# Loading the taps of a 3x3 convolution onto other partitions: four transfers of two taps for am, two for an, some to every second partition

## The chip, the cores and the metric

The kernel runs on one core of a Trainium2 chip. The metric is device time in microseconds of one execution. Five engines matter here: TensorE (PE, with its weight loads PEld), VectorE (DVE), ScalarE (ACT), GpSimd (POOL) and SyncE (SP), which only starts transfers. All transfers are carried by the core's 16 DMA engines.

## What is computed

Four images of 16 channels, 256 x 256, float32, pass through two layers. Each layer adds to its input a function of the group-normalised input (`_gn`, 8 groups).

```python
# layer 0
out = conv3x3(gn(x), conv_w) + conv_b            # 16 -> 400 channels: 16 channels x 25 logits
w   = softmax(out.reshape(N, 16, 25, H, W), axis=2)
x   = x + sum over the 25 taps of unfold5x5(gn(x)) * w
# layer 1
x   = x + silu(patches3x3(gn(x))) @ base_w + b_splines(patches3x3(gn(x))) @ spl_w + bias
```

The change is in layer 0, in how the operands of the 3x3 convolution reach the chip's memory.

## The kernel before, in words

**Setup (0 to 110 us).** The images are read once for their statistics. Meanwhile the first half of image 0 is normalised and written to DRAM three times: as `hs` (rows, for the 5x5 window), as `hst` (columns, float32) and as `hsl`, which holds for each channel two planes `[C, 2, CT]`: the value rounded to float32r (`hi`) and what the rounding lost (`lo`). `prepare0` lays out the weights: `wm` (float32, 128 rows: 8 of the 9 taps x 16 channels) and `wn` (float32r, 97 rows: the ninth tap, and the bias).

**Layer 0 (110 to 2021 us).** There are 64 strips of 32 image columns (`SW`), each worked through in 4 tiles of 8 columns (`CI`), so 256 tiles; and a tile in 2 units of 4 columns (`JG`), so 512 units.

- For each tile `load_im` starts on SP three transfers into `am` (lines 717 to 724: 48, 48 and 32 partitions, each row a run of 1038 floats) and two into `an` (lines 727 to 734: 32 partitions each, the 16 channels times hi and lo, the same source twice). The rows of `am` are 8 shifted copies of 16 channels. Rows 64 to 96 of `an` hold ones (line 706), which multiply the bias rows of `wn`.
- For each column PE multiplies 128 rows of `am` by `wm` (line 922) and 97 rows of `an` by `wn` (line 926) into the same PSUM bank `lg` (400 logits).
- ACT takes the exponential of two columns at a time (line 945) into `e`.
- POOL multiplies `e` by the 5x5 window `u` (line 950), one instruction per unit.
- DVE sums both over the 25 taps (line 771), one instruction per unit. Per strip it then makes the quotient (lines 791, 795, 799, with ACT's Ln and Exp at 785 and 787), and POOL subtracts it from `xc` (line 805).
- After every four strips ACT starts two stores of 1 MB each, `x1s<-xc` (line 862), in rows of 512 bytes; there are 15 such pairs on ACT, the last is on POOL.
- Between the units, steps of `normalize` prepare the next image in the same way (transposes at line 402, ACT's copies, `lo` on DVE at line 414, the writes at lines 323 and 337).

**What sets the order.** The program of each engine is fixed when it is built. `load_im(k + 2)` stands at the start of tile k; `am` has three buffers, so the load of a tile waits until PE has finished the tile three before. SP is one queue in order: `am`, `an`, `u` (five transfers a strip, line 743), `xc` (line 749), `xp` (line 315) and the writes stand behind each other. In the built program every transfer of SP and of ACT carries one of eight completion semaphores, taken in turn in program order, ACT's stores included. A transfer is not started until the last one on its semaphore, eight places earlier, has landed. So SP has at most eight transfers in flight, and the pair of stores holds two of the eight places until it has landed.

**Layer 1 (2021 to 2912 us)** reads `x1s` and is not touched.

Of the kernel before, what the change touches and what calls it, by code (L numbers as in the profile page):

```python
# [34 lines left out]
def conv_preact_kernel(  # L35
# [32 lines left out]
    LAG = 1  # L68
    RP = P + 2
    CT = (W + 2) * RP  # L70
    QC = 4
    QW = W // (P // QC)
    QG = 4
# [26 lines left out]
    ident = const.tile([P, P], F32, name="ident")  # L100
# [7 lines left out]
    for k, d in enumerate((0, RD - 1)):  # L108
        h = k * (P // 2)
# [142 lines left out]
    zero = const.tile([PAD * C, max(RP, NST * SP)], F32, name="zero")  # L252
    nc.vector.memset(zero, 0.0)

    zpad = const.tile([P, QC, PAD], F32, name="zpad")
    nc.vector.memset(zpad, 0.0)

    def zeros(b, queue):

        for e in (0, HP - PAD):  # L260
            for r in range(PAD):
                yield partial(
                    queue.dma_start,
                    hs[b][:, e + r].rearrange("s c w -> c s w"),
                    zero[0:C, 0 : NST * SP].rearrange("c (s w) -> c s w", s=NST),
                )
        yield partial(
            queue.dma_start,
            bass.AP(
                tensor=x1s[b].tensor, offset=x1s[b].offset,  # L270
                ap=[[CP, C], [(H + 1) * W, 2], [1, W]],
            ),
            zero[0 : 2 * C, 0:W],
        )
        for h in range(NH):
            for w in (0, (W + 1) * RP):
                yield partial(queue.dma_start, hst[b][h][:, w : w + RP], zero[0:C, 0:RP])
                yield partial(
                    queue.dma_start,
                    hsl[b][h][:, :, w : w + RP].rearrange("c t r -> (c t) r"), zero[:, 0:RP],  # L280
                )


# [2 lines left out]
    kept = [  # L286
        const.tile([P, C // QC * NQ, QG, 1], d, name=f"kept{i}") for i, d in enumerate((F32, F32R, F32R))
    ]

    def normalize(b, ptr, tiles, held=None, copier=None, part=None, dense=False):  # L290
# [22 lines left out]
        def load(q, h):  # L313
            if held is None and q < C // QC:
                nc.sync.dma_start(
# [13 lines left out]
        def put_columns(q, n):  # L329
            g0 = n * QG  # L330
            for h in parts:

                for to, ti, t in ((hst, 0, tts[n]), (hsl, 0, his[n]), (hsl, 1, los[n])):
                    d = to[b][h]
                    m = 2 if to is hsl else 1
                    t = t if t.dtype == F32 else t.bitcast(F32)
                    nc.sync.dma_start(
                        bass.AP(
                            tensor=d.tensor,
                            offset=d.offset + q * QC * m * CT + ti * CT + (1 + g0) * RP,  # L340
                            ap=[[QW * RP, W // QW], [m * CT, QC], [1, QG * RP]],
                        ),
                        t[:, h].rearrange("p g r -> p (g r)"),
                    )
# [115 lines left out]
    with tc.tile_pool(name="prep0", bufs=2) as prep, tc.tile_pool(  # L460
        name="pre", bufs=1
    ) as pre, tc.tile_pool(
        name="xin", bufs=3
    ) as xin, tc.tile_pool(name="stat", bufs=2) as stat, tc.tile_pool(
        name="pstat", bufs=1, space=PSUM
# [16 lines left out]
        loaded = [load_x(n) for n in range(5)]  # L482

        wr = pre.tile([P, NL], F32, name="wr")
        for dj in range(3):
            v = conv_wt[dj].rearrange("(d c) n -> c d n", d=3)
            nc.sync.dma_start(
                wr[dj * 3 * C : min((dj + 1) * 3 * C, P), :], v[:, 0 : 3 if dj < 2 else 2, :]
            )
        wnr = pre.tile([KT, NL], F32, name="wnr")  # L490
        nc.vector.memset(wnr, 0.0)
        v = conv_wt[2, 2 * C : 3 * C]
        for r in (0, 2 * C):
            nc.sync.dma_start(
                wnr[r : r + 2 * C, :],
                bass.AP(tensor=v.tensor, offset=v.offset, ap=[v.ap[0], [0, 2], [1, NL]]),
            )
        for r in (4 * C, 6 * C):
# [4 lines left out]
        for d in range(3):  # L503
# [3 lines left out]
            v = spl_s[dc]  # L507
# [23 lines left out]
        def prepare0():  # L531

            def places(t):
                return t.rearrange("p (c m d) -> p m c d", c=C, m=K)

            wp = pre.tile([KT, K, C, K], F32, name="wp")
            for m in range(K):
                nc.gpsimd.tensor_copy(wm[:, m], places(wr)[:, m])
                nc.gpsimd.tensor_copy(wp[:, m], places(wnr)[:, m])
            whi = pre.tile([KT, K, C, K], F32R, name="whi")  # L540
# [13 lines left out]
            nc.vector.memset(times[0 : 4 * C], 0.25)  # L554
            nc.vector.memset(times[4 * C : 4 * C + 1], 1.0)
# [41 lines left out]
        for b in range(B):  # L597
            st = stat.tile([P, G, NH * (GC if b == 0 else 1), 6], F32, name=f"st0_{b}", tag=f"st0{min(b, 1)}")
            for hf in range(NH):
                n = b * NH + hf  # L600
                t = loaded.pop(0)
# [33 lines left out]
            v = hm[:, b * NH : (b + 1) * NH]  # L635
# [55 lines left out]
    def layer0(shift):  # L691
# [4 lines left out]
        with tc.tile_pool(name=f"prep{arm}", bufs=2) as prep, tc.tile_pool(  # L696
            name=f"im{arm}", bufs=NIM
        ) as imp, tc.tile_pool(name=f"l0{arm}", bufs=2) as l0, tc.tile_pool(
            name=f"nd{arm}", bufs=3
        ) as ndp, tc.tile_pool(name=f"x1{arm}", bufs=3) as x1p, tc.tile_pool(name=f"ptr{arm}", bufs=1, space=PSUM) as ptr, tc.tile_pool(  # L700
            name=f"plog{arm}", bufs=3, space=PSUM
        ) as plog, tc.tile_pool(name=f"prc{arm}", bufs=1, space=PSUM) as prc:
            ans = [imp.tile([KT, CI * RP], F32R, name=f"an{n}{arm}", bufs=1) for n in range(NIM)]
            for t in ans:

                nc.vector.memset(t.bitcast(F32)[4 * C : KT], 1.0)
            tiles = norm_tiles(prep)
            strips = [(b, hf, s) for b in range(B) for hf in range(NH) for s in range(NST)]
            nci = SW // CI
# [1 line left out]
            def load_im(n):  # L711
                b, hf, s = strips[n // nci]
                j0 = s * SW + n % nci * CI
                run = CI * RP - 2
                am = imp.tile([P, CI * RP], F32, name=f"am{n}{arm}", tag="am")
                d = hst[b][hf]
                for dj in range(3):
                    nd = 3 if dj < 2 else 2
                    nc.sync.dma_start(
                        am[dj * 3 * C : dj * 3 * C + nd * C, 0:run],  # L720
                        bass.AP(
                            tensor=d.tensor, offset=d.offset + (j0 + dj) * RP,
                            ap=[[CT, C], [1, nd], [1, run]],
                        ),
                    )
                an = ans[n % NIM]
                d = hsl[b][hf]
                for r in (0, 2 * C):
                    nc.sync.dma_start(
                        an.bitcast(F32)[r : r + 2 * C, 0:run],  # L730
                        bass.AP(
                            tensor=d.tensor, offset=d.offset + (j0 + 2) * RP + 2,
                            ap=[[CT, 2 * C], [1, run]],
                        ),
                    )
                return am, an
# [118 lines left out]
            def store(n, xc):  # L855
# [5 lines left out]
                for h in range(2):  # L861
# [7 lines left out]
                    name=nc.get_next_instruction_name(), engine=mybir.EngineType.Activation,  # L869
# [10 lines left out]
            for n, (b, hf, s) in enumerate(strips):  # L880
# [22 lines left out]
                nd = ndp.tile([P, 2, C, SW], F32, name=f"nd_{n}{arm}", tag="nd")  # L903
                for j in range(0, SW, JG):
                    if j % CI == 0:
                        k = n * nci + j // CI
                        if k + 2 < len(strips) * nci:
                            ims.append(load_im(k + 2))
                        am, an = ims.pop(0)
# [8 lines left out]
                    for j1 in range(0, JG, 2):  # L918
# [28 lines left out]
                        tensor=u.tensor, offset=u.offset + j,  # L947
                        ap=[u.ap[0], [1, JG], [SP, K * C], [1, K]],
# [436 lines left out]
```

## Time and profile before

| | us |
|---|---|
| median of 4 runs | 2912.2 |
| lowest, highest run | 2910.28, 2913.88 |
| profiled execution, its own time | 2913.87 |
| its span (first to last instruction) | 2912.0 |
| setup, up to the first transfer of layer 0 | 109.6 |
| last convolution matmul starts | 2021.0 |
| transfers of am: 512 of 194.6 KB, 256 of 129.8 KB | SP issue, median 0.587 |
| transfers of an: 512 of 129.8 KB | SP issue, median 0.422 |

The profile is of one execution. A group's row gives line, engine, operation, output<-inputs, count, busy time, mean duration, and the idle time just before its instructions with what ended it. A row of the table by stretches gives for each engine the busy time in that stretch and the number of instructions, then the granted TensorE clock (1.00 is full), the mean busy share of the 16 DMA engines (it can exceed 1 in a short stretch, because a packet is booked where it ends) and the GB/s that they moved.

### The profile page before, as it was taken

How to read it: one execution, taken by the hardware profiler on the slowest of the kernel's cores; microseconds unless marked ns; L12 is line 12 of the kernel's file. 1: busy time of each engine (PE TensorE's matmuls, PEld its weight loads, DVE VectorE, ACT ScalarE, POOL GpSimd, SP SyncE). 2: the span in 40 equal slices, each digit the busy share in tenths (PEclk: the TensorE clock that was granted, in tenths of full speed). 3: DMA queues.
4: the chain of work that ended last, by engine and by line, in shares of the span. 5: the costliest groups of instructions: out<-in, count | busy, mean ns of one | idle time of the engine just before them, and what ended most of it. 6: DMA issues, size and time to landing. Idle time of an engine off the chain costs nothing.

```text
span 2912.0 us, 40991 instructions
## 1 busy us (share of the span) xinstructions
PE 2719.1 (93%) x14282; PEld 1507.5 (52%) x14282; DVE 2803.6 (96%) x1866; ACT 2124.8 (73%) x2764; POOL 2704.1 (93%) x1117
## 2 busy tenths in 40 slices
PE   4699999999999999999999999997799999999998
PEld 3466656666666656656656656664243343333232
DVE  6599999999999999999999999999899999999996
ACT  6466876667767558676655655647899999999995
POOL 4299999999999999999999999999899999999995
PEclk7799999999999999999999999999899999999999
DMA  9898999889889688888976757766788788787883
GB/s 283 242 247 229 258 250 269 238 216 241 234 235 256 192 218 235 236 236 233 252 205 172 201 160 195 193 173 176 247 245 259 243 256 250 243 263 240 256 249 101
DMA packets 403467, 664.43 MB, mean 228 GB/s; under 512 B 43186, under 2 KB 267908, under 8 KB 387380
## 3 DMA queue, kind: packets, MB, share of 16 engines
q1 hardware_dynamic: 339284, 626.53, 76.6%
q10 hardware_dynamic: 61920, 31.46, 3.8%
q0 software_dynamic: 2048, 3.72, 0.4%
q8 instruction: 117, 1.92, 0.3%
q14 instruction: 98, 0.80, 0.1%
HBM read 532.96 MB, written 121.15 MB: 225 GB/s over the span
## 4 chain that ended last, share of the span: by engine, by line
DVE 44%; PE 27%; DMA 9%; ACT 7%; issue 6%; POOL 5%; SPq 2%; DVEq 0%; ACTq 0%; POOLq 0%
DVE nd L771 32%; PE lg L922 12%; PE yp L1252 9%; PE lg L926 3%; DVE ring L175 3%; POOL e L950 3%; DVE s L172 3%; PE yp L1261 2%; DMA an<-hsl 2%; DMA x1s<-xc 2%; DVE r1a L1096 1%; ACT xta L1087 1%; DMA xin<-in_x_dram 1%; ACT xtb L1087 1%; DMA xta<-x1s 1%
## 5 line engine op out<-in xcount | busy, mean ns | idle before, releaser
L950 POOL TENSOR_TENSOR e<-e,u 128x1600 f32<-128x1600 f32 x512 | 1788.8, 3544 | 54.4 <-ACT e L945 40.1
L922 PE MATMUL lg<-wm,am 128*128 128x400 f32 x4096 | 1736.6, 505 | 74.8 <-ACT e L945 36.7
L771 DVE TENSOR_REDUCE nd<-e 128x128 f32<-128x3200 f32 x512 | 1760.7, 3484 | 34.6 <-POOL e L950 34.1
L926 PE MATMUL lg<-wn,an 97*128 97x400 f32 x2048 | 1344.2, 656 | 15.0 <-DMA an<-hsl 14.8
L945 ACT ACTIVATE e<-lg 128x800 f32<-128x800 f32 x1024 | 834.5, 839 | 580.4 <-PE lg L926 329.2
L922 PEld LDWEIGHTS lg<-wm,am 128*128 128x128 f32 x4096 | 763.7, 192 | 387.5 <-ACT e L945 70.1
L1252 PE MATMUL yp<-ring,wt 128*32 128x512 f32 x6144 | 721.1, 595 | 35.4 <-DVE ring L175 34.9
L926 PEld LDWEIGHTS lg<-wn,an 97*128 97x128 f32 x2048 | 388.6, 190 | 336.5 <-DMA an<-hsl 25.2
L1252 PEld LDWEIGHTS yp<-ring,wt 128*32 128x32 f32 x6144 | 234.4, 109 | 485.9 <-issue 397.2
L1109 POOL TENSOR_TENSOR s1b<-s1b,r1a 128x1024 f32<-128x1024 f32 (+1 forms) x96 | 192.5, 2038 | 0.0
L1109 POOL TENSOR_TENSOR s1a<-s1a,r1a 128x1024 f32<-128x1024 f32 (+1 forms) x96 | 192.1, 2032 | 0.0
L175 DVE SCALAR_TENSOR_TENSOR ring<-s,s1a 128x1024 f32<-128x1024 f32 x132 | 156.7, 1211 | 0.9
L825 ACT ACTIVATE z<-xc,nrm 128x256 f32<-128x256 f32 x240 | 144.0, 600 | 18.2 <-POOL xc L805 14.2
L175 DVE SCALAR_TENSOR_TENSOR ring<-s,s1b 128x1024 f32<-128x1024 f32 (+1 forms) x128 | 153.6, 1225 | 0.3
L1109 POOL TENSOR_TENSOR s1a<-s1a,r1b 128x512 f32<-128x512 f32 (+2 forms) x68 | 119.4, 1781 | 0.0
L1109 POOL TENSOR_TENSOR s1b<-s1b,r1b 128x512 f32<-128x512 f32 x64 | 114.8, 1819 | 0.0
L1105 POOL TENSOR_TENSOR s1a<-r1b 128x1536 f32<-128x1536 f32 (+1 forms) x31 | 86.6, 2793 | 28.3 <-ACT r1b L1094 28.3
L172 DVE SCALAR_TENSOR_TENSOR s<-xta,cb,s 128x1024 f32<-128x1024 f32 (+2 forms) x90 | 112.3, 1274 | 0.3 <-DMA sla<-x1s 0.2
L172 DVE SCALAR_TENSOR_TENSOR s<-xtb,cb,s 128x1024 f32<-128x1024 f32 (+2 forms) x85 | 107.1, 1287 | 3.8 <-ACT s L169 3.8
L172 DVE SCALAR_TENSOR_TENSOR s<-xtc,cb,s 128x1024 f32<-128x1024 f32 (+2 forms) x85 | 107.0, 1286 | 0.0
L169 ACT ACTIVATE s<-xta,cb 128x1024 f32<-128x1024 f32 (+2 forms) x90 | 96.4, 1085 | 12.4 <-DVE ring L175 10.8
L1105 POOL TENSOR_TENSOR s1b<-r1b 128x1536 f32<-128x1536 f32 (+1 forms) x32 | 86.3, 2698 | 18.6 <-ACT r1b L1094 18.6
(209 smaller groups left out, 2313.1 us busy)
## 6 DMA issues: line engine op xcount, KB each, us to landing
am<-hst SPq DMA_DIRECT2D x512, 194.6 KB
u<-hs SPq DMA_DIRECT2D x320, 288.0 KB
an<-hsl SPq DMA_DIRECT2D x512, 129.8 KB
xta<-x1s SPq DMA_DIRECT2D x40, 1024.0 KB
xtb<-x1s SPq DMA_DIRECT2D x40, 1024.0 KB
xtc<-x1s SPq DMA_DIRECT2D x40, 1024.0 KB
am<-hst SPq DMA_DIRECT2D x256, 129.8 KB
x1s<-xc ACTq DMA_DIRECT2D x30, 1024.0 KB
```

The lines of the kernel that those rows point to most:

```text
L169: nc.scalar.activation(s, t, AF.Square, scale=-0.5, bias=cb)
L172: nc.vector.scalar_tensor_tensor(p, t, cb2, s, ALU.subtract, ALU.mult)
L175: nc.vector.scalar_tensor_tensor(f, p, 0.0, q, ALU.min, op)
L771: nc.vector.tensor_reduce(nd[:, :, :, j : j + JG].rearrange("p t c j -> p t j c"), e.rearrange("p t j m c d -> p t j c m d"), AX.XY, ALU.add,)
L825: nc.scalar.activation(z, v, f, scale=nrm[b][:, 0, g : g + 1], bias=nrm[b][:, 1, g : g + 1], accum_out=st1[b][:, t, g, columns_of(n) : col ...
L922: nc.tensor.matmul(lg[:, i, :NL], lhsT=am[:, o : o + P], rhs=wm.rearrange("p m c d -> p (m c d)"), start=True, stop=False,)
L926: nc.tensor.matmul(lg[:, i, :NL], lhsT=an[:, o : o + P], rhs=wn.rearrange("p m c d -> p (m c d)"), start=False, stop=True,)
L945: nc.scalar.activation(ev, lg[:, :, :NL], AF.Exp)
L950: nc.gpsimd.tensor_tensor(e[:, 1].rearrange("p j m c d -> p j (m c) d"), e[:, 0].rearrange("p j m c d -> p j (m c) d"), uv, ALU.mult,)
L1105: nc.gpsimd.tensor_tensor(s1(n, a, z), r1(n, a, z), r1(n, a, z), ALU.mult)
L1109: nc.gpsimd.tensor_tensor(s1(n, a, z), s1(n, a, z), r1(n, a, z), ALU.mult)
L1252: nc.tensor.matmul(yp[t * M : (t + 1) * M], lhsT=wt[:, d, e].rearrange("p r o -> p (r o)"), rhs=ring[:, r0 + t * RT + d : r0 + t * RT + d ...
```

## The change

`am` is loaded by four transfers of two taps (32 partitions each) where there were three of 48, 48 and 32. The first goes to partitions 0 to 31, the third to 96 to 127, the second and the fourth to the even and the odd ones of 32 to 95. `an` still takes two transfers of 32 partitions, now to the even and the odd partitions of 32 to 95, and its ones are rows 0 to 31; it has 96 rows, not 97. `hsl` has a pitch of 2 CT + 16 floats for each channel, so that its source keeps a dimension of 16 channels and one of 2 planes. The rows of the weights and of the bias follow: `wr` is loaded by four transfers, `wnr` by two of another shape, and `wn` is made by two instructions on DVE (a rounding copy, and `whi * odd + wp`, where `odd` is -1 on odd partitions), where it took one on DVE and three on ACT. In layer 0 the number of instructions on PE, ACT, POOL and DVE is unchanged; SP starts six transfers for each tile, not five.

```diff
+    CL = 2 * CT + 16
...
-    hsl = [[dram.tile([C, 2, CT], F32, name=f"hsl{b}_{h}") for h in range(NH)] for b in range(B)]
+    hsl = [[dram.tile([C, CL], F32, name=f"hsl{b}_{h}") for h in range(NH)] for b in range(B)]
...
-    KT = 6 * C + 1
+    KT = 6 * C
+    TAPS = (
+        (slice(0, 2 * C), (0, 0), (0, 1)),
+        (slice(2 * C, 6 * C, 2), (1, 0), (0, 1)),
+        (slice(6 * C, P), (0, 2), (1, 0)),
+        (slice(2 * C + 1, 6 * C, 2), (2, 0), (0, 1)),
+    )
...
             whi = pre.tile([KT, K, C, K], F32R, name="whi")
-            nc.scalar.copy(whi, wp)
-            nc.vector.tensor_sub(wn, wp, whi.bitcast(F32))
-            nc.scalar.copy(wn[0 : 2 * C], wp[0 : 2 * C])
-            nc.scalar.copy(wn[4 * C : 4 * C + 1], wp[4 * C : 4 * C + 1])
+            nc.vector.tensor_copy(whi, wp)
+            nc.vector.scalar_tensor_tensor(
+                wn, whi.bitcast(F32), odd[0:KT], wp, ALU.mult, ALU.add
+            )
...
-                nc.vector.memset(t.bitcast(F32)[4 * C : KT], 1.0)
+                nc.vector.memset(t.bitcast(F32)[0 : 2 * C], 1.0)
...
-                for dj in range(3):
-                    nd = 3 if dj < 2 else 2
+                for rows_, at, step in TAPS:
                     nc.sync.dma_start(
-                        am[dj * 3 * C : dj * 3 * C + nd * C, 0:run],
+                        am[rows_, 0:run],
                         bass.AP(
-                            tensor=d.tensor, offset=d.offset + (j0 + dj) * RP,
-                            ap=[[CT, C], [1, nd], [1, run]],
+                            tensor=d.tensor, offset=d.offset + (j0 + at[0]) * RP + at[1],
+                            ap=[[CT, C], [step[0] * RP + step[1], 2], [1, run]],
                         ),
                     )
                 an = ans[n % NIM]
                 d = hsl[b][hf]
-                for r in (0, 2 * C):
+                for k in range(2):
                     nc.sync.dma_start(
-                        an.bitcast(F32)[r : r + 2 * C, 0:run],
+                        an.bitcast(F32)[2 * C + k : 6 * C : 2, 0:run],
                         bass.AP(
                             tensor=d.tensor, offset=d.offset + (j0 + 2) * RP + 2,
-                            ap=[[CT, 2 * C], [1, run]],
+                            ap=[[CL, C], [CT, 2], [1, run]],
                         ),
                     )
```

More of the change, by code (lines that the diff above doesn't have):

```diff
@@ L279, in zeros @@
                     queue.dma_start,
-                    hsl[b][h][:, :, w : w + RP].rearrange("c t r -> (c t) r"), zero[:, 0:RP],
+                    hsl[b][h][:, 0 : 2 * CT].rearrange("c (t w) -> c t w", t=2)[:, :, w : w + RP],
+                    zero[:, 0:RP],
                 )
@@ L334, in put_columns @@
                     d = to[b][h]
-                    m = 2 if to is hsl else 1
+                    pitch = CL if to is hsl else CT
                     t = t if t.dtype == F32 else t.bitcast(F32)
@@ L339, in put_columns @@
                             tensor=d.tensor,
-                            offset=d.offset + q * QC * m * CT + ti * CT + (1 + g0) * RP,
-                            ap=[[QW * RP, W // QW], [m * CT, QC], [1, QG * RP]],
+                            offset=d.offset + q * QC * pitch + ti * CT + (1 + g0) * RP,
+                            ap=[[QW * RP, W // QW], [pitch, QC], [1, QG * RP]],
                         ),
@@ L484, in conv_preact_kernel @@
         wr = pre.tile([P, NL], F32, name="wr")
-        for dj in range(3):
-            v = conv_wt[dj].rearrange("(d c) n -> c d n", d=3)
+        for rows_, at, step in TAPS:
             nc.sync.dma_start(
-                wr[dj * 3 * C : min((dj + 1) * 3 * C, P), :], v[:, 0 : 3 if dj < 2 else 2, :]
+                wr[rows_],
+                bass.AP(
+                    tensor=conv_wt.tensor,
+                    offset=conv_wt.offset + (at[0] * 3 + at[1]) * C * NL,
+                    ap=[[NL, C], [(step[0] * 3 + step[1]) * C * NL, 2], [1, NL]],
+                ),
             )
@@ L492, in conv_preact_kernel @@
         v = conv_wt[2, 2 * C : 3 * C]
-        for r in (0, 2 * C):
+        for r in (2 * C, 4 * C):
             nc.sync.dma_start(
                 wnr[r : r + 2 * C, :],
-                bass.AP(tensor=v.tensor, offset=v.offset, ap=[v.ap[0], [0, 2], [1, NL]]),
+                bass.AP(
+                    tensor=v.tensor, offset=v.offset + (r // C - 2) // 2 * (C // 2) * NL,
+                    ap=[[NL, C // 2], [0, 4], [1, NL]],
+                ),
             )
-        for r in (4 * C, 6 * C):
+        for r in range(2):
             nc.sync.dma_start(wnr[r : r + 1, :], conv_b)
@@ L539, in prepare0 @@
                 nc.gpsimd.tensor_copy(wp[:, m], places(wnr)[:, m])
+            odd = pre.tile([P, 1], F32, name="odd")
+            nc.vector.reduce_sum(odd, ident[:, 1:P:2], AX.X)
+            nc.vector.tensor_scalar(odd, odd, -1.0, None, ALU.mult)
             whi = pre.tile([KT, K, C, K], F32R, name="whi")
-            nc.scalar.copy(whi, wp)
-            nc.vector.tensor_sub(wn, wp, whi.bitcast(F32))
-            nc.scalar.copy(wn[0 : 2 * C], wp[0 : 2 * C])
-            nc.scalar.copy(wn[4 * C : 4 * C + 1], wp[4 * C : 4 * C + 1])
+            nc.vector.tensor_copy(whi, wp)
+            nc.vector.scalar_tensor_tensor(
+                wn, whi.bitcast(F32), odd[0:KT], wp, ALU.mult, ALU.add
+            )
             aw = pre.tile([P, 2, NL], F32, name="aw")
@@ L553, in prepare0 @@
             nc.vector.memset(times, 0.0)
-            nc.vector.memset(times[0 : 4 * C], 0.25)
-            nc.vector.memset(times[4 * C : 4 * C + 1], 1.0)
+            nc.vector.memset(times[2 * C : 4 * C], 0.25)
+            nc.vector.memset(times[4 * C : 6 * C], 0.25)
+            nc.vector.memset(times[0:1], 1.0)
             nc.tensor.matmul(wps, lhsT=onec, rhs=aw[:, 0], start=True, stop=False)
@@ L716, in load_im @@
                 d = hst[b][hf]
-                for dj in range(3):
-                    nd = 3 if dj < 2 else 2
+                for rows_, at, step in TAPS:
                     nc.sync.dma_start(
-                        am[dj * 3 * C : dj * 3 * C + nd * C, 0:run],
+                        am[rows_, 0:run],
                         bass.AP(
-                            tensor=d.tensor, offset=d.offset + (j0 + dj) * RP,
-                            ap=[[CT, C], [1, nd], [1, run]],
+                            tensor=d.tensor, offset=d.offset + (j0 + at[0]) * RP + at[1],
+                            ap=[[CT, C], [step[0] * RP + step[1], 2], [1, run]],
                         ),
@@ L727, in load_im @@
                 d = hsl[b][hf]
-                for r in (0, 2 * C):
+                for k in range(2):
                     nc.sync.dma_start(
-                        an.bitcast(F32)[r : r + 2 * C, 0:run],
+                        an.bitcast(F32)[2 * C + k : 6 * C : 2, 0:run],
                         bass.AP(
                             tensor=d.tensor, offset=d.offset + (j0 + 2) * RP + 2,
-                            ap=[[CT, 2 * C], [1, run]],
+                            ap=[[CL, C], [CT, 2], [1, run]],
                         ),
```

## The prediction

> **What bounds the kernel now.** I read the page first, for each engine's share and its dearest groups; then layer 0 in stretches, to see which engine has no time left; then the waits of that engine and of the one before it.
>
> ```profile
> PE 2719.1 (93%) x14282; PEld 1507.5 (52%) x14282; DVE 2803.6 (96%) x1866; ACT 2124.8 (73%) x2764; POOL 2704.1 (93%) x1117
> ...
> L950 POOL TENSOR_TENSOR e<-e,u 128x1600 f32<-128x1600 f32 x512 | 1788.8, 3544 | 54.4 <-ACT e L945 40.1
> ...
> L771 DVE TENSOR_REDUCE nd<-e 128x128 f32<-128x3200 f32 x512 | 1760.7, 3484 | 34.6 <-POOL e L950 34.1
> ```
>
> One unit costs POOL 3.544 us and DVE 3.484; with what each strip adds, both are near full. The stretches of layer 0 (after the span and the PE and PEld columns comes DVE, then ACT, POOL, clock, DMA share, GB/s):
>
> ```profile
> 110.00:150.00 40.00, 31.27 (x95) 19.66 (x96) 20.90 (x10) 16.58 (x23) 21.81 (x15) 0.82 1.01 241
> 150.00:500.00 350.00, 337.42 (x1213) 219.69 (x1211) 348.97 (x148) 248.17 (x432) 338.98 (x104) 0.99 0.93 250
> 500.00:900.00 400.00, 385.95 (x1364) 249.84 (x1363) 398.78 (x163) 269.64 (x463) 393.65 (x123) 0.99 0.86 233
> 900.00:1300.00 400.00, 378.21 (x1317) 243.17 (x1315) 396.60 (x161) 261.46 (x458) 386.94 (x121) 0.98 0.86 229
> 1560.00:1990.00 430.00, 409.72 (x1412) 263.67 (x1410) 424.87 (x186) 242.10 (x390) 429.37 (x142) 0.99 0.71 186
> ```
>
> After 150 us DVE is busy 99% of the time, and after 1560 POOL is (429.37 of 430). DMA is full only at the start. The waits of DVE and POOL from 150 to 1990 say how much a faster load can return at all:
>
> ```profile
> DVE nd L771 <- POOL e L950: 15.6, 15, 2.5
> ...
> POOL e L950 <- ACT e L945: 35.6, 21, 6.1
> ```
>
> DVE idles 15.6 us in 1840, and 18.8 us more before 150. So whatever the change does to the DMA engines, layer 0 can gain 34 us at the very most, and only where these idle times come from loads.
>
> **What a tile's load costs now.** Two stretches, one with only `u` in flight (128 partitions), one with only `am` and `an` (32 to 48), and the SP rows of that tile:
>
> ```profile
> 1898.00:1900.50 2.50, 2.50 (x11) 1.61 (x10) 2.50 (x2) 1.56 (x2) 2.50 (x2) 1.00 1.06 393
> 1908.00:1910.00 2.00, 2.00 (x8) 1.27 (x7) 2.00 (x3) 1.29 (x2) 2.00 (x2) 1.00 1.03 237
> ```
> ```profile
> 1905.76 1.81 SPq L719 DMA_DIRECT2D am<-hst  x3
> 1907.67 0.99 SPq L729 DMA_DIRECT2D an<-hsl  x2
> ```
>
> The DMA engines are full in both, yet move 393 GB/s in one and 237 in the other, though the rows of `am` are longer (4152 bytes against 2304). The number of partitions is the difference that I see. A tile is 2 x 194.6 + 129.8 + 2 x 129.8 = 778.6 KB, 797 kB, so 3.36 us at 237 GB/s. **After:** six transfers of 132.9 kB. Those to 32..95 in steps of two spread over 64 partitions. If these four go at 393 and the other two at 237: 4 x 0.34 + 2 x 0.56 = 2.47 us, 0.9 less. Bounds: all six at 393 is 2.03 us, 1.3 less; nothing gained, and the sixth transfer adding its issue time of 0.60, is 0.6 more. I take 0.9, since `u` with 288 KB a transfer is the nearest row to an unshared load.
>
> The trace shows that few partitions are slow, not which partitions share a way in. The Trainium skill, "SBUF — State Buffer", section "Door 1: The DMA port swizzle", says which: 0 to 31 reach 8 of 16 ports, 0 to 63 the same 8, 64 to 127 the others; so rows 32 to 95 reach all 16, and two rows for each DMA engine, four partitions apart from the next engine's, would give each its own port. Against the change stands the same page's "The DMA setup-cost knee": each transfer pays some 2 us, and few large ones are better. By that, paid in turn, 256 more transfers would be an estimate of 512 us; the five transfers that take 3.36 us together at a DMA share of 1.03 say that it isn't paid in turn.
>
> SP: three transfers 1.81 us, 0.60 each, with a source of three dimensions; two 0.99, 0.50 each, with two. Now all have three: 4 x 0.60 + 2 x 0.60 = 3.6 us against 2.8, so 0.8 more a tile, 205 us in all. Its cover:
>
> ```profile
> SPq L719 <- PE lg L926: 475.9, 180, 5.8
> ...
> SPq L729 <- DMA x1s<-xc: 73.1, 10, 14.5
> SPq L719 <- DMA x1s<-xc: 65.2, 17, 11.1
> ```
>
> SP waits 476 us for PE to release buffers, twice what is added. Where that cover is gone (SP catching up), 0.8 us a tile shows and takes back the 0.9. Behind a late issue stand `u`, `xc` and the writes of `normalize`.
>
> **Step 1, setup.** ACT loses three instructions on `whi` and `wn` (0.51, 0.52 and 0.53 us at 53 to 57 us), DVE gets two for one (nearest row: its `wn` at 55.56, 0.55 us). ACT is busy 10.00 of 10 us from 60 to 70 and from 70 to 80, and SP's last image load (issued at 80.13, landed at 91) stands behind ACT's work; the chain of waits runs through `ACT wn L544`. All of it returned is -1.6; DVE's two on the chain instead, +1.1. I take -1.0. One more `wr` transfer stands behind image loads that take to 37 us, and `wm` is first touched at 44: nothing.
>
> **Step 2, the start, 110 to 150.** Before the first matmul stand one more issue of 0.60 and two of 0.1: PE starts 0.8 later. But DMA is the bound here (1.01), and DVE's second stall (4.57 us at 137) comes from ACT, which waits 5.51 us in order for `xp` to land at 135.45, behind two further tiles in the queue. 2 x 0.9 less: -1.8, and the later start disappears in that stall. Ends: +0.8 (loads no faster), -3.5 (three tiles at 1.3 are 3.9, less some issue).
>
> **Step 3, the rest of layer 0.** I went through DVE's idle times one by one.
> - At 468 to 475 (0.9), 824 to 839 (1.2) and 1303 to 1318 (2.6) they end a catch-up: DMA share 1.04 from 786 to 821, in which SP starts five tiles. 5 x 0.9 = 4.5 us of the 4.8 and 6.1 that POOL idles there. I take 3.8 of the 4.7 as returned.
> - At 1041 to 1050 (3.2) and 1520 to 1528 (2.5) SP was held by a pair of stores:
>
> ```profile
> 1015.54 2.15 ACTq L862 DMA_DIRECT2D x1s<-xc  x2
> 1020.74 0.52 SPq L337 DMA_DIRECT2D hst<-tt  x1
> 1024.43 1.86 SPq L719 DMA_DIRECT2D am<-hst  x3
> 1030.42 1.67 PE L922 MATMUL lg<-wm,am 128*128 128x400 f32 x2 [6.13 <-DMA am<-hst]
> 1037.78 7.00 POOL L950 TENSOR_TENSOR e<-e,u 128x1600 f32<-128x1600 f32 x2 [6.13 <-ACT e L945]
> ```
>
> SP goes on at 1020.74, when the first store has landed, and at 1024.43 after the second; only then is the tile's load started. In the changed program one write more is held until the second store (0.6), and the six issues take 0.8 longer; the data come 0.9 sooner. I count 0.
> - From 1716 to 1737 (4.9) POOL is busy throughout and sets the pace: 0.
> - **New holds.** In the program before, at 7 of the 15 pairs the first store holds an `an` load of the next tile, the second only an `am` of the tile after. In the changed program there the second store holds the next tile itself. At 1620.48 `an` is issued after the first store and lands at 1626.8; after the second (the `am` row from 1622.13 takes 4.66 us, its last two issues 1.2 of it, so about 1625.6) and with nothing beside it, landing 2.3 us after issue (as at the start: 113.64 to 115.9), it would be 1627.9: 1.1 late. ACT's exponentials were then only 0.2 to 0.4 us ahead of POOL (done at 1632.22 for a unit that starts at 1632.6), after the store at 1853 2.5 us. Four of these pairs lie where POOL sets the pace. I take +1.0 in all; ends 0 and 7 x 3.7 = 26 (the 3.7 us between 1020.74 and 1024.43, uncovered).
>
> Step 3: -3.8 + 1.0 = -2.8. **Sum: -1.0 - 1.8 - 2.8 = -5.6 us**, so 2908.3 for the profiled execution (2913.87: span 2912.0 and 1.9 around it). The median is 1.7 below that execution, so 2906.6. Layer 1 is untouched.
>
> **Rivals.**
> 1. *The cover is gone everywhere.* The catch-ups and the holds vanish too, and all of setup and start comes back: -1.6 - 3.5 - (15.6 - 4.9) = -15.8, 2896.4. For it: DMA work falls by 256 x 0.9 = 230 us. Against it: the holds are no matter of bandwidth (DMA stood still from 1012 to 1016).
> 2. *The loads get no faster*, since rows or queues and not partitions make 237 GB/s: start +0.8, setup -1.0, catch-ups +0.8 a tile on SP, some 3 us: 2915. Against it: the row at 393 with shorter rows.
> 3. *Slower: the stores hold the next tile.* Place: the seven pairs. It decides once the second store lands over 2.5 us (the larger margin seen) after PE needs the tile. Price 7 x (1.1 to 3.7) = 8 to 26, less the 6.6 of steps 1, 2 and the catch-ups that stay: +1 to +19, middle 2922. For it: ACT's margin of 0.2 to 0.4 us at 1632. Against it: earlier pairs have DVE, not POOL, as the pace, with 1 us more of margin.
>
> **How the numbers follow.** Forecast (2903 to 2910) 0.52; rival 1 (2894 to 2903) 0.16; rival 2 (2911 to 2916) 0.15; rival 3 (2914 to 2932) 0.17. About 0.2% (5.8 us, to 2906.4) is what a measurement can tell from no change; half of the forecast's range lies past it. Faster: 0.26 + 0.16 = 0.42; same: 0.26 + 0.15 = 0.41; slower: 0.17. The range leaves out the far half of rival 3 and the lowest of rival 1: 2896 to 2919.
>
> **What would show it.** With only `am` and `an` in flight: 300 GB/s or more at a share of 1 (wrong if 237). Six issues in 3.6 us. DVE's wait for POOL from 150 to 1990 about 12 us; at 820 and 1300 none, at 1040 and 1520 still there. `xp` landing 1 to 2 us sooner after the first load. The last image load issued near 79. If POOL waits for ACT after 1560 at each fourth strip, rival 3 is at work; if `an` is what PE waits for there, by these holds.

## The result, and the profile after

The changed kernel takes **2914.7 us** (median of 33 runs, 2910.81 to 2920.51) where the kernel before takes 2910.6 (53 runs): a ratio of 1.0012, 95% interval 1.0008 to 1.0017. The forecast was a gain of 5.6 us; it is a loss of 4.1. The profiled execution of the changed kernel took 2917.7 us (span 2915.4), against 2913.9 (2912.0).

The page's two dearest groups after the change:

```profile
L968 POOL TENSOR_TENSOR e<-e,u 128x1600 f32<-128x1600 f32 x512 | 1789.5, 3550 | 61.1 <-ACT e L963 47.2
...
L789 DVE TENSOR_REDUCE nd<-e 128x128 f32<-128x3200 f32 x512 | 1761.2, 3481 | 38.5 <-POOL e L968 37.6
```

The work of one unit is what it was (3.55 and 3.48 us). The idle time in front of it has grown, from 54.4 to 61.1 us on POOL and from 34.6 to 38.5 on DVE. Three of the stretches of layer 0 (columns as before: PE, PEld, DVE, ACT, POOL, clock, DMA share, GB/s; a packet's whole time is booked in the stretch in which the packet starts):

```profile
150.00:500.00 350.00, 334.02 (x1198) 217.88 (x1198) 345.69 (x147) 245.12 (x429) 335.72 (x104) 0.99 0.83 247
500.00:900.00 400.00, 386.71 (x1347) 251.18 (x1345) 394.66 (x162) 267.88 (x459) 388.98 (x122) 0.97 0.77 231
...
1560.00:1990.00 430.00, 411.10 (x1401) 263.66 (x1400) 423.66 (x185) 241.62 (x384) 427.46 (x141) 0.98 0.63 182
```

The DMA engines move about as many GB/s as before (247, 231 and 182 for 250, 233 and 186), in less busy time: the share falls from 0.93, 0.86 and 0.71 to 0.83, 0.77 and 0.63. That looks as hoped, but `c_contig` below, without the spread, shows the same fall. And DVE has lost 3.3 us in the first stretch and 4.1 in the second. Its waits from 150 to 1990, POOL's, and those of SP's own queue from 110 to 2010 (total, times, longest):

```profile
DVE nd L789 <- POOL e L968: 20.2, 19, 3.4
DVE lo L422 <- ACT hi L405: 1.8, 1, 1.8
```
```profile
POOL e L968 <- ACT e L963: 43.8, 31, 5.6
```
```profile
SPq L737 <- PE lg L944: 288.2, 153, 5.2
SPq L737 <- DMA x1s<-xc: 132.9, 15, 15.6
...
SPq L747 <- DMA x1s<-xc: 18.6, 10, 5.5
```

DVE waits 22.0 us where it waited 15.6. SP's time to spare (its wait for PE to release buffers) has gone from 476 to 288 us. The holds by stores of `x1s` have moved from `an` to `am`: 132.9 us on `am` and 18.6 on `an`, where it was 65.2 and 73.1. In all they grew little: with the other transfers, SP waits 177.9 us in layer 0 for the thirty stores that ACT starts, where it waited 169.6.

**Where the time went.** The starts of DVE's 64 strips, after minus before, show it. Setup gained 4.25 us (first `am` issue at 105.34, was 109.59), the start another 1.3 (strips 2 to 10 are 5.6 early). Then strips 10 to 12 lose 3.4, 14 to 16 lose 1.6, 22 to 24 lose 2.5, 58 to 63 lose 1.6, with small gains near 1042 and 1520: layer 0 ends 2.6 late. So **layer 0 lost 8.2 us** after the start, where I had forecast a gain of 2.8. Each of the first three losses lies behind a pair of `x1s` stores.

One pair of executions is a coarse measure, though. `a_weights` below has the layer 0 of before, and in its trace layer 0 gains 4.5 us on the same trace of before. By the medians the changed kernel is 0.21% slower than `a_weights`, which shares the new way of making `wn`: the loads alone cost some 6 us (3 to 9 by the two intervals).

**What a tile's load became.** The stretch with only `am` and `an` in flight, and the SP rows of that tile:

```profile
1912.00:1915.00 3.00, 3.00 (x13) 1.97 (x12) 2.92 (x2) 1.67 (x2) 3.00 (x2) 1.00 0.75 208
```
```profile
1910.29 2.46 SPq L737 DMA_DIRECT2D am<-hst  x4
1912.85 1.17 SPq L747 DMA_DIRECT2D an<-hsl  x2
```

Before, the engines were full (1.03) at 237 GB/s. Now they are three quarters full at 208. SP takes 3.73 us for the six issues, 0.62 each, and each brings 132.9 kB: 132.9 / 0.62 = 214 GB/s is all that SP asks for. In these rows the tile has moved from a DMA bound of 3.36 us to an SP bound of 3.73.

The Trainium skill, "DMA: Bandwidth & Descriptors", section "Issuing engines are not separate DMA queues", calls the sequencer's time to start a DMA usually small beside the DMA itself. Here it isn't: 0.62 us of SP against 0.56 (132.9 kB at the 237 GB/s seen before), and the measurement decides.

One catch-up shows both halves. The stores of the fifth pair are issued at 777.06 before and at 777.11 after. SP's rows behind them, before and then after:

```profile
771.37 12.83 SPq L719 DMA_DIRECT2D am<-hst  x3
784.30 2.56 SPq L729 DMA_DIRECT2D an<-hsl  x2
```
```profile
782.37 4.53 SPq L737 DMA_DIRECT2D am<-hst  x4
787.00 1.17 SPq L747 DMA_DIRECT2D an<-hsl  x2
```

Before, one of the tile's three `am` transfers was out before the hold (771.37), and the second started after it, at 782.25. After, all six wait for the first store (782.37), and the last of the four `am` transfers for the second. Then both catch up:

```profile
786.00:821.00 35.00, 28.59 (x96) 17.47 (x94) 35.00 (x16) 22.81 (x46) 29.10 (x10) 0.95 1.04 277
```
```profile
786.00:821.00 35.00, 28.82 (x89) 18.25 (x88) 35.00 (x16) 21.61 (x42) 29.92 (x10) 0.86 0.86 259
```

Before, the DMA engines are full (1.04) and bring 277 GB/s; after, they are at 0.86 and bring 259. SP's issues fill 31.3 of these 35 us, where they filled 25.9: it has little time left to ask for more. At 826.65 DVE waits 3.43 us for POOL, where it had waited 0.91 at 824.

### The profile page after: what moved, and what is told of

Read it like the earlier page. It is cut to its first block, busy times and chain, and to the rows that moved or that the text cites. A ratio compares the mean times of both kernels' runs of the same rounds, so it can differ in the third digit from the quotient of the medians.

```text
span 2915.4 us, 41250 instructions
## 1 busy us (share of the span) xinstructions
PE 2722.9 (93%) x14282; PEld 1497.4 (51%) x14282; DVE 2805.6 (96%) x1870; ACT 2126.8 (73%) x2761; POOL 2704.4 (93%) x1117
## 4 chain that ended last, share of the span: by engine, by line
PE 40%; DVE 33%; DMA 7%; issue 7%; ACT 6%; POOL 5%; SPq 1%; DVEq 0%; ACTq 0%; POOLq 0%
DVE nd L789 25%; PE lg L940 16%; PE yp L1270 15%; POOL e L968 5%; PE lg L944 5%; PE yp L1279 4%; DVE ring L182 2%; DVE s L179 2%; DMA x1s<-xc 2%; DMA am<-hst 1%; ACT e L963 1%; DMA xin<-in_x_dram 1%; DVE r1a L1114 1%; DMA an<-hsl 1%; DVE r L813 1%
## 5 line engine op out<-in xcount | busy, mean ns | idle before, releaser
L968 POOL TENSOR_TENSOR e<-e,u 128x1600 f32<-128x1600 f32 x512 | 1789.5, 3550 | 61.1 <-ACT e L963 47.2
L789 DVE TENSOR_REDUCE nd<-e 128x128 f32<-128x3200 f32 x512 | 1761.2, 3481 | 38.5 <-POOL e L968 37.6
L944 PE MATMUL lg<-wn,an 96*128 96x400 f32 x2048 | 1351.9, 660 | 7.7 <-DMA an<-hsl 7.5
L944 PEld LDWEIGHTS lg<-wn,an 96*128 96x128 f32 x2048 | 390.2, 191 | 326.8 <-issue 23.7
L1270 PEld LDWEIGHTS yp<-ring,wt 128*32 128x32 f32 x6144 | 224.2, 109 | 500.4 <-issue 413.0
```

The costliest lines, as they stand in the source:

```text
L789: nc.vector.tensor_reduce(nd[:, :, :, j : j + JG].rearrange("p t c j -> p t j c"), e.rearrange("p t j m c d -> p t j c m d"), AX.XY, ALU.add,)
L944: nc.tensor.matmul(lg[:, i, :NL], lhsT=an[:, o : o + P], rhs=wn.rearrange("p m c d -> p (m c d)"), start=False, stop=True,)
L968: nc.gpsimd.tensor_tensor(e[:, 1].rearrange("p j m c d -> p j (m c) d"), e[:, 0].rearrange("p j m c d -> p j (m c) d"), uv, ALU.mult,)
L1270: nc.tensor.matmul(yp[t * M : (t + 1) * M], lhsT=wt[:, d, e].rearrange("p r o -> p (r o)"), rhs=ring[:, r0 + t * RT + d : r0 + t * RT + d ...
```

## Experiments

Theories at first: **N**, the number of transfers a tile (SP's issue time, and how soon a store holds the next tile); **S**, setup gains some 4 us because the weights are split on DVE; **P**, the rows spread over 32 to 95 make a load cheaper; and as a rival **T**, the spread itself costs. Later N was divided into **Q**, SP's issue time, and **H**, which load the stores hold (as **H2**: how many loads of the next tile they hold). Ratios are to the kernel before, run beside, with 95% intervals.

**a_weights**: the kernel before, with `wn` made by two DVE instructions; loads unchanged.

```
-            nc.scalar.copy(whi, wp)
-            nc.vector.tensor_sub(wn, wp, whi.bitcast(F32))
-            nc.scalar.copy(wn[0 : 2 * C], wp[0 : 2 * C])
-            nc.scalar.copy(wn[4 * C : 4 * C + 1], wp[4 * C : 4 * C + 1])
...
+            nc.vector.tensor_copy(whi, wp)
+            nc.vector.scalar_tensor_tensor(
+                wn, whi.bitcast(F32), low[0:KT], wp, ALU.mult, ALU.add)
```

> The kernel before with one part of the change alone: wn is made by two instructions on DVE (a rounding copy and whi * low + wp, low being -1 on the rows that take the rest), no longer by three on ACT and one on DVE. Loads and layout are those of before. In the trace of after, layer 0's first transfer is issued at 105.3 us, 4.3 earlier than before. Theory S (the move of these instructions shortens setup): first transfer of layer 0 near 105 to 106, and since nothing in layer 0 differs, 4 us less than before: ratio 0.9980 to 0.9988. Rival (setup got shorter for another reason: the weight transfers, or how the scheduler placed the rest): first transfer near 109.6 and a ratio of 0.9995 to 1.0005.

2905.7 us, ratio 0.9991 (0.9982 to 1.0000), just outside the range of S; the first `am` issue at 105.64, where S had it. So S holds, but for some 3 us and not 4: the three traces with the old setup (before, `q_before_drain`, `n_before_store3`) have that issue at 109.59, 108.47 and 108.26, the fifteen with the new one at 104.75 to 106.83, on average 3.0 us earlier.

**b_an_alone**: the changed kernel with the three `am` transfers of before (five a tile).

```
-                for rows_, at, step in TAPS:
+                for dj in range(3):
...
```

> After, with the three transfers of am of before (48, 48, 32 partitions); an goes to every second partition as in after. Five transfers a tile, so the turn of the eight semaphores is that of before. Theory N (the sixth transfer cost layer 0 its gain: SP needs 3.7 us a tile instead of 2.9, and the pairs of stores hold the next tile's load earlier): layer 0 stalls no more than before, DVE waits for POOL 16 us or less from 150 to 1990, and with the shorter setup 2903 to 2907, ratio 0.9975 to 0.999. Rival T (the spread rows themselves cost time: they land later or slow others): DVE's waits near 20 us as in after and a ratio of 1.000 to 1.002.

2908.2 us, ratio 0.9998 (0.9990 to 1.0007). DVE waits 15.4 us from 150 to 1990, as N had it (T: near 20), but N's range of time is missed by a little. Against the trace of before DVE starts 4.4 us early, has given back 3.7 of it by strip 12, and ends layer 0 3.9 early.

**c_contig**: the changed kernel, each of the six transfers to 32 adjacent rows, and the rows of the weights to match.

```
-        (slice(2 * C, 6 * C, 2), (1, 0), (0, 1)),
+        (slice(2 * C, 4 * C), (1, 0), (0, 1)),
...
```

> After, with all six transfers a tile to 32 partitions side by side (am to 0-31, 32-63, 96-127, 64-95 in the order of after; an to 32-63 and 64-95); rows of weights to match. Count, form, order and semaphores of the transfers are those of after; only the spread is undone. Theory P (spread makes a tile's load cheaper, 2.5 us instead of 3.4, and this hides a part of the sixth transfer's cost): with only am and an in flight the rate falls back to 220 to 250 GB/s at a share of 1, the catch-ups after the stores get longer, 2917 to 2930, ratio 1.002 to 1.007 to before. Rival T (the spread is what costs): faster than after, ratio 0.998 to 1.000. If neither, within 1 us of after (1.001 to 1.002), the catch-ups are bound by SP alone.

2918.3 us, ratio 1.0035 (1.0023 to 1.0047): slower than the changed kernel by 0.23%, 6.7 us, with the same load held at each of the thirty stores. T falls, and the spread is worth something; by which way is not shown (in the two traces layer 0 ends 2.8 us apart, 1.6 of it by strip 2). But the tile's load looks as it did with the spread, and so does the DMA share over the first stretch (0.83 there):

```profile
1914.00:1917.00 3.00, 3.00 (x13) 1.94 (x11) 3.00 (x2) 1.67 (x2) 3.00 (x2) 1.00 0.73 204
```
```profile
150.00:500.00 350.00, 335.75 (x1199) 218.49 (x1197) 345.29 (x147) 245.29 (x429) 335.20 (x103) 0.98 0.84 247
```

So the lower DMA share does not come from the spread, and the lighter load that the prediction hoped for from it shows with adjacent rows too. The Trainium skill, "SBUF — State Buffer", section "Door 1: The DMA port swizzle", has 32 adjacent rows reach half of the ports; the 0.23% between these two kernels goes that way, but at the 204 to 208 GB/s that SP asks for, no run here could show what all ports would carry.

**d_an_one**: `b_an_alone` with `an` as one transfer to rows 32 to 95 (four a tile), and `hsl` without the 16 floats more of pitch.

```
-                for k in range(2):
-                    nc.sync.dma_start(an.bitcast(F32)[2 * C + k : 6 * C : 2, 0:run], ...)
+                nc.sync.dma_start(an.bitcast(F32)[2 * C : 6 * C, 0:run], ...
+                        ap=[[CT, 2 * C], [0, 2], [1, run]])
```

> The last but one kernel (am by three transfers as before, an spread) with the two transfers of an made one: 64 partitions, 32 to 95 side by side, each of hi and lo twice from one source row (hsl without the pitch of 16 more). Four transfers a tile, each an row where after has it. Theory N: SP needs 2.4 to 2.6 us a tile, a pair of stores holds SP about one tile later, so fewer stalls than with five: DVE waits under 12 us from 150 to 1990, 2898 to 2904, ratio 0.996 to 0.998. Rival: the count does not matter, the same as with five within 1 us.

**2896.5 us, ratio 0.9961 (0.9948 to 0.9974)**: the fastest of all, 0.4% under before. DVE's waits from 150 to 1990, and the SP rows of a tile:

```profile
DVE nd L785 <- POOL e L964: 6.0, 5, 2.1
```
```profile
1909.93 1.81 SPq L734 DMA_DIRECT2D am<-hst  x3
1911.84 0.55 SPq L743 DMA_DIRECT2D an<-hsl  x1
```

SP needs 2.46 us a tile, and DVE waits 6.0 us instead of 22.0. Against `a_weights`, with `wn` made in the same way, the gain is 0.30%.

**e_after_an_one**: the changed kernel with that one `an` (five a tile, 3.1 us of SP).

> The changed kernel, but an is loaded by one transfer to the 64 rows 32 to 95 (five transfers a tile, some 3.1 us of SP, against six and 3.7; the four am transfers are as changed). Theory N (the number of transfers a tile decides, whichever they are): as b_an_alone, which has five too: 2904 to 2910, ratio 0.998 to 1.000. Theory P (the am rows laid over all of 32 to 95 are worth something once SP has time): 2895 to 2902, near or below d_an_one with its 2896.5. If it is over 2912, splitting am by two taps is bad by itself.

2900.8 us, ratio 0.9976 (0.9965 to 0.9986). P's range, not N's: 0.22% under `b_an_alone`, with as many transfers and as much SP time. So the number alone is not the rule. Which rows a transfer covers may count too, by as much as between c_contig and the changed kernel, but the sizes of the transfers and the loads that the stores hold differ as well here. The first stretch shows the DMA share of the changed kernel, with 0.6 us less of SP a tile:

```profile
150.00:500.00 350.00, 336.57 (x1211) 219.54 (x1209) 349.24 (x148) 245.14 (x429) 338.92 (x104) 0.99 0.83 251
```

**h_d_drain**: `d_an_one` with a pause on SP; no transfer is added or moved.

```
+                for _ in range(4):
+                    nc.sync.drain()
                 an = ans[n % NIM]
```

> d_an_one (four transfers a tile) with four empty drain instructions on SP between the am and the an load of each tile: SP takes longer for a tile, the transfers and which of them the stores hold are those of d_an_one. The pause is read from the trace. Theory Q (SP's issue time in the catch-ups is the price of the sixth transfer): if the pause brings SP's time for a tile to 3.5 us or more, 2905 to 2915; with a pause under 0.5 us, 2897 to 2901. Theory H (the price is that the stores hold the next tile's loads and not those of the tile after): within 3 us of d_an_one's 2896.5 for any pause up to 1.5 us.

```profile
1906.12 1.81 SPq L734 DMA_DIRECT2D am<-hst  x3
1908.61 0.55 SPq L745 DMA_DIRECT2D an<-hsl  x1
```

From the end of `am` to the start of `an` it is now 0.68 us, where `d_an_one` has 0.10: a pause of 0.59 us a tile. 2905.4 us, ratio 0.9990 (0.9981 to 0.9999): 0.29%, 8.4 us, over `d_an_one`. The transfers and their order on SP are the same. The expectation had the holds the same too, and they are not: in the built program the pauses moved the stores among the semaphores, and at 22 of the 30 stores the load that waits stands one or two places earlier in SP's order. At the fifth pair, for `d_an_one` and then here (the first row takes in the wait for the first store):

```profile
773.64 0.55 SPq L743 DMA_DIRECT2D an<-hsl  x1
...
778.11 1.82 SPq L734 DMA_DIRECT2D am<-hst  x3
```
```profile
768.20 10.90 SPq L734 DMA_DIRECT2D am<-hst  x3
...
782.71 0.33 SPq L314 DMA_DIRECT2D hst<-zero  x1
```

In `d_an_one` the stores hold the `an` of this tile and the next tile's `am`; here they hold the last `am` of this tile and a write. SP waits 164.2 us for the stores in layer 0, where it waited 133.7. So this run alone does not tell Q from H; `p_after_u_one` and `r_after_drain` below do.

**i_d_hold**: `d_an_one` with two tiny transfers on ACT's queue behind each pair of stores, so that the stores hold earlier loads.

```
+                    for k in range(...):
+                        nc.scalar.dma_start(spare[...], xc[0:1, 0, 0:64])
```

> d_an_one with two 256-byte transfers on ACT's queue behind each pair of x1s stores (one behind the second pair, none behind the seventh and eleventh), written to a spare array that nobody reads. They take two of the eight completion semaphores, so that the first store again holds loads of the very next tile, as before and after the change; SP's issues are those of d_an_one. Theory H (the hold of the next tile decides): 2903 to 2911, with DVE waits after the store pairs again, 12 to 18 us in all. Theory Q (SP's issue time decides): 2895.5 to 2899, DVE's wait near d_an_one's 6.0 us. ACT's 26 further issues cost some 0.5 us each on an engine with 25% to spare.

```profile
ACT e L963 <- DMA spare<-xc: 31.7, 5, 6.5
```

2926.7 us, ratio 1.0065 (1.0051 to 1.0079). ACT itself had to wait 31.7 us in front of its exponentials for these transfers: the run tells nothing of H.

**k_d_u_one**: `d_an_one` with the five loads of `u` made one.

```
-                for m in range(K):
-                    nc.sync.dma_start(u[:, m], hs[b][s, r0 : r0 + P])
+                nc.sync.dma_start(..., ap=[w.ap[0], [w.ap[0][0], K], w.ap[1]])
```

> d_an_one with the five loads of u made one (source of three dimensions, five overlapping runs for each row): 17 loads a strip where d_an_one has 21 and the changed kernel 29. By both theories fewer is better still: 2891 to 2896, at most the 6.0 us that DVE still waits after 150 us and some of the start. If it is slower than d_an_one, one transfer of 1440 KB holds am and an behind it longer than five of 288 KB do, and the number alone is not the rule.

2898.2 us, ratio 0.9964 (0.9951 to 0.9978), as `d_an_one`: where a tile needs 2.46 us of SP, less gives nothing more.

**m_after_store3, m_after_store4, n_before_store3, o_d_store3, s_d_store1**: the stores of `x1s` one or two units later (in the last one earlier) in the program.

```
-                        after(2, store, n, xc)
+                        after(3, store, n, xc)
```

> The changed kernel with each pair of x1s stores put one unit (some 3.5 us) later in the program. In the order of the program the eighth transfer after each store, which is the one that has to wait for it, is then the same load as in the kernel before (am of tile 42 and an of 42 for the second pair, where the changed kernel had the first and the last am of 42). Theory H (the holds decide): what the changed kernel lost in layer 0 comes back and setup's gain stays: 2902 to 2906, ratio 0.998 to 0.9995. Theory Q (SP's 3.7 us for a tile decides, at whatever hold): 2910 to 2915, ratio 1.0005 to 1.002, DVE's wait still some 20 us.

> The changed kernel with the x1s stores two units later: the stores now hold no load of the next tile but those of the tile after or of a third, as in d_an_one or later still. Theory H: as d_an_one, 2895 to 2901, ratio 0.995 to 0.9975. Theory Q: still 2909 to 2915. Both by halves: 2902 to 2908.

> The kernel before with the x1s stores one unit later: each store holds the same loads as in d_an_one (tile 59's am and an for the third pair, where the kernel before had an of 58 and am of 59), with five transfers a tile, 2.8 us of SP, the setup and the rows as before. Theory H: d_an_one's gain without its setup (some 4 us): 2898 to 2903, ratio 0.997 to 0.9985. Theory Q (SP 2.8 us as before): 2905 to 2909, ratio 0.9995 to 1.0005.

> d_an_one with the x1s stores one unit later: holds later still (a load two tiles on or three). Theory H: DVE's 6.0 us of waiting shrink further, 2891 to 2896. Theory Q: as d_an_one, 2895 to 2898. Slower than 2898 if the later store itself costs something (xc kept longer, or a store beside the loads of u).

> d_an_one with the x1s stores one unit (3.5 us) earlier: they land earlier, and hold loads half a tile earlier in the program (am of 57 and 58 for the third pair, where d_an_one had am and an of 59). One unit later had cost 12.5 us (o_d_store3). If the landing time alone decides, a gain: 2885 to 2895. If landing and need move together, as d_an_one: 2894 to 2900. If the load held first is now one that PE needs at once, slower: 2900 to 2912.

Ratios: m_after_store3 1.0105 (1.0089 to 1.0120), m_after_store4 1.0024 (1.0015 to 1.0033), n_before_store3 1.0058 (1.0045 to 1.0072), o_d_store3 0.9999 (0.9990 to 1.0008), s_d_store1 1.0007 (0.9998 to 1.0016). Neither theory foresaw it: **one unit later costs** 0.9% on the changed kernel, 0.6% on the one before and 0.4% on `d_an_one`, one unit earlier 0.5% there, and two units later only 0.1% on the changed kernel. H in my form, that the load named by the order of the program decides, falls. In `o_d_store3` the first store of the fifth pair is issued at 773.91, not 768.41, and SP is free again at 779.11, not 773.64: the held load is needed later, but the store lands as much later. SP's wait for the stores in layer 0 grew in the four slow runs (177.9 to 202.7 us for m_after_store3, 169.6 to 198.8 for n_before_store3, 133.7 to 146.7 and to 179.4 for o_d_store3 and s_d_store1); in m_after_store4 it fell to 143.3, and nothing was gained. What counts may be the time from the landing of a store to the need of the load that waits for it; no run varies it alone, and these runs do not tell how much of the change's loss it is.

**p_after_u_one**: the changed kernel with the edit of `k_d_u_one`; `am` and `an` as changed.

> The changed kernel with the five loads of u made one: SP issues four transfers fewer in each strip (some 1.9 us of 17.2), am and an as changed. Theory Q (SP's time in the catch-ups is the price; the pause of 0.59 us a tile cost h_d_drain 8.9 us over d_an_one): 1.9 us a strip is 0.47 us a tile, so some 7 us back: 2905 to 2909, ratio 0.998 to 0.9995. If only the tile next behind a store counts (theory H2: how many loads of that tile the stores hold), nothing: 2911 to 2916.

2908.2 us, ratio 0.9992 (0.9983 to 1.0001): 1.9 us less of SP in a strip gives back 0.20%, 5.8 us, where the same edit gave `d_an_one` nothing. DVE waits 16.7 us, not 22.0:

```profile
DVE nd L792 <- POOL e L971: 15.3, 16, 2.2
DVE lo L422 <- ACT hi L405: 1.4, 1, 1.4
```

Here the holds stayed: at each of the thirty stores the load that waits is that of the changed kernel, and SP waits 179.3 us for them, where it was 177.9. So this is SP's time: **1.9 us of SP a strip, 0.47 a tile, is worth 5.8 us**. Q has a price of its own, and H2 falls as the whole account.

**q_before_drain** and **r_after_drain**: the pause of `h_d_drain` in the kernel before and in the changed one.

> The kernel before with the pause of h_d_drain (four empty drains, 0.59 us a tile) between am and an: SP 3.4 us a tile in place of 2.8, loads, rows and holds as before. Theory Q: 6 to 11 us slower than before, 2914 to 2920, ratio 1.002 to 1.004, which is what the changed kernel lost in layer 0 (7 to 8 us). Theory H2: within 2 us of before. If it is over 1.006, SP's time costs more the nearer it comes to a tile's load time of 3.4 us.

> The changed kernel with the same pause: SP 4.3 us a tile. Theory Q: 8 to 13 us slower than the changed kernel, 2921 to 2928, ratio 1.004 to 1.007, as SP alone now paces each catch-up (a tile of work is 6.9 us). Theory H2: within 2 us of the changed kernel's 2914.7.

q_before_drain 2914.1 us, ratio 1.0015 (1.0006 to 1.0024); r_after_drain 2923.4, ratio 1.0040 (1.0027 to 1.0054), 0.28% over the changed kernel.

```profile
DVE nd L791 <- POOL e L970: 28.5, 22, 4.1
```

In r_after_drain DVE waits these 28.5 us and 2.3 for ACT. Here the tile grows by less than the pause, since the issues of `an` behind it got shorter: from 2.9 to 3.27 us in q_before_drain, which costs 4.4 us (the loads' 3.36 may hide part of it), and from 3.73 to 4.29 in r_after_drain, which costs 8. The holds moved a little again: 18 of 30 are the same in both, 9 are earlier and 3 later in q_before_drain, 1 is earlier and 11 are later in r_after_drain. There SP waits less for the stores than in the changed kernel (160.2 us, not 177.9), so longer holds do not explain the loss. All by the time that SP needs for a tile:

| kernel | transfers a tile | SP, us a tile | ratio |
|---|---|---|---|
| d_an_one | 4 | 2.46 | 0.9961 |
| before (old setup) | 5 | 2.9 | 1 |
| a_weights | 5 | 2.9 | 0.9991 |
| h_d_drain | 4 | 3.04 | 0.9990 |
| e_after_an_one, b_an_alone | 5 | 3.1 | 0.9976, 0.9998 |
| q_before_drain (old setup) | 5 | 3.27 | 1.0015 |
| changed; rows adjacent (c_contig) | 6 | 3.73 | 1.0012; 1.0035 |
| p_after_u_one (1.9 less a strip for `u`) | 6 | 3.73 | 0.9992 |
| r_after_drain | 6 | 4.3 | 1.0040 |

The order is rough: around 3 us a tile the ratios go from 0.9976 to 0.9998, so SP's time is not all.

## Why the prediction was wrong

- **The bound** (DVE, then POOL, near full): right. After 150 us the 15.6 us of waits were the whole room for a gain; they grew to 22.0.
- **The tile's load, 2.47 us: this is the step that failed.** The prediction had 3.6 us of SP for the six issues and 2.47 us of DMA side by side, and took the gain from the smaller. A tile can't load faster than it is asked for. Measured: 3.73 us of SP, DMA at a share of 0.75, 208 GB/s. It says "Where that cover is gone (SP catching up), 0.8 us a tile shows and takes back the 0.9", and in step 3 it then counts 5 x 0.9 as returned in the very catch-ups, where SP hardly waits for PE. An estimate of the price: SP needs 0.83 more a tile (3.73 less 2.90); p_after_u_one got 5.8 us for 0.47 and r_after_drain lost 8 for 0.56, which makes 10 to 12 us. With adjacent rows the loss against `a_weights` is 0.44%, 12.8 us, and with the spread, which gives 6.7 back, 6. Step 3 had -2.8.
- **The reason for the 2.47, the partitions:** not borne out. The busy time of the DMA engines did fall, but as much with 32 adjacent rows (0.84 at 247 GB/s) as with the spread (0.83 at 247). At the 204 to 208 GB/s that SP asks for, no run shows what rate the spread rows would allow.
- **The cover of 476 us**: a sum over layer 0, and right as a sum (288 are left). But no cover carries over from one tile to the next behind a hold, and most of the holds that were on `an` now stop a tile at its `am` (132.9 us on `am` for 65.2).
- **The holds.** Of the seven pairs that I named (+1.0) the first, which is the third of all, cost 1.6 us. The others show little: strips 24 to 58 shift by -1.4 in all, and POOL waits for ACT 1.8 us after 1560. The pairs that cost were the second, third and fifth. At the second, fifth and ninth the first store holds the whole next tile now, where one of its `am` transfers was out before; the prediction had not gone through these.
- **Setup, -1.0**: it is -4.25 between these two traces, and some -3.0 over all of them (see `a_weights`). The right mechanism, mis-sized: I counted ACT's three instructions and not the wait in front of one, which the row in the trace of before had in its brackets:

```profile
56.15 0.52 ACT L543 CAST wn<-wp 32x400 fp32r<-32x400 f32 x1 [1.47 <-DVE wn L542]
```

  With 1.56 of work that is 3.0; ACT's last square of an image starts 3.13 earlier (87.89 for 91.02). The last image load is issued at 76.90, not near 79.
- **The start, -1.8**: -1.3, as reasoned; `xp` lands 1.4 us sooner after the first load.
- **The rivals.** The second has the right number (2915 for 2914.7), in part by luck: it is counted from a median of 2912.2, the change is measured from 2910.6, so it said +2.8 where +4.1 came. It has the right term, 0.8 a tile on SP, but not the right cause of slow loads: it had rows or queues that can't go faster, and it is SP that doesn't ask. The signs that I named in advance did their work: 300 GB/s were not seen, DVE's wait rose where 12 us were forecast, and the stalls at 820 and 1300 stayed (3.43 and 2.36 us).

**Open**: how the loss of layer 0 is shared between SP's issue time and the moved holds, and how the spread gives its 6.7 us back. SP's time is shown to act with the holds unchanged, by p_after_u_one, and by the estimate it is large enough by itself. Moving the stores is shown to cost, but whether by the loads that they hold is not.

## What to carry to other kernels

A queue's issue time is a bandwidth: bytes of a transfer over the time of an issue. Before a load is split for the sake of the engines behind it, set the issue time of all parts beside the transfer time, take the larger, and do so where the queue is catching up, not over the whole stage. Here four transfers a tile were 0.3% faster than five (`d_an_one` against `a_weights`), and six 0.2% slower. And when a pause or an edit is to leave something as it was, here the holds, read from its trace that it did.

## What the runs showed of the hardware that I had not expected

- One issue of SP took 0.59 us (median of `am`) or 0.54 (`an`) with a source of three dimensions, and in a row they brought 132.9 kB every 0.62 us, 214 GB/s. An estimate from this: to keep up the 237 GB/s seen before, a transfer must have 147 kB (237 x 0.62). One transfer of twice the size, with each row of the source repeated by a step of zero, was issued in 0.55 us.
- For about the same GB/s the busy share of the DMA engines went with the form of the transfers and hardly with SP's pace. From 150 to 500 us it was 0.93 before (`am` by three), 0.88 in d_an_one (`am` by three, `an` by one; 2.46 us of SP a tile) and 0.87 in h_d_drain (3.04), but 0.83 both in e_after_an_one (`am` by four; 3.1) and in the changed kernel (3.73), all at 247 to 251 GB/s. Why is not shown.
- Four empty drains on SP took 0.59 us, steadily (0.68 to 0.70 us from `am` to `an` in nine of ten tiles of h_d_drain, 0.10 without them). They also moved the stores among the semaphores in the built program.
- A pair of stores half a tile earlier or later moved the whole by 11 to 27 us, 0.4 to 0.9%; a whole tile later (the changed kernel), by 3.5.
